# A decoder layer on one core: the first expert's rows, the last batch's norm, the experts' roots and the last gathers moved or rewritten

## The chip, the core and the metric

The kernel runs on one core of one Trainium2 chip. The metric is the time of one execution on the device in microseconds (us), as the median of a few runs. The engines are named as in the profile: PE is TensorE (PEld its weight loads), DVE is VectorE, ACT is ScalarE, POOL is GpSimd, and SP is the sync engine, whose queue issues most of the plain transfers. Every engine takes its own instructions in the order in which they stand in its queue. Durations below come from one profiled execution.

## The reference

The layer has 16 batches of 256 tokens of width 256, all in float32. It has three parts, each followed by a residual sum and a layer norm. The part that the change touches is the third, and the end of the second:

```
# 2: cross attention of the tokens (after norm 1) to 77 context rows and to themselves, 8 heads of 128
sim = q @ k.T ; attn = softmax(sim) ; out = (attn @ v) @ Wo + bo
x = layernorm(x + out)
# 3: experts: each token picks its 2 best of 8 experts; an expert takes its first 512 tokens
dot = x @ embeddings.T ; weights = softmax over the top 2
for each expert e: y = relu(x_e @ first[e].T) @ second[e].T * weight ; final[tokens of e] += y
x = layernorm(x + final)
```

The first part is a recurrence over the sequence with a short convolution ahead of it. It is not touched.

## The kernel before, in words

**Attention.** A loop runs over 128 pairs of batch and head, `(b, h)`, as a software pipeline (L875 to L891). In step i it makes keys and queries of head i (`head_kq`, matmuls `pk`, `pq`), runs the small jobs that a table `steps` has put at that head, multiplies probabilities and values of head i-2 (`head_out`, `po`, L484), makes scores and softmax of head i (`head_softmax`, `s`, L448: a maximum on DVE, two exponentials on ACT, a reciprocal L456 and two scalings L459 on DVE), and transposes the probabilities of head i-1 (`head_turn`, `pa` and `pb`, L471, copied to SBUF by DVE at L473 and by ACT at L474).

**What the table puts where.** At the heads of batch b, the table places the end of batch b-1: the two projections (`project`, `pw`, L502, one per 128 tokens, eight matmuls each), with bias, residual and norm behind the second one (L511 to L516), the transposes of its tokens (`turn_tokens`, `px`), the expert scores (`score_experts`, `pl`, L544), the choice of two experts (`choose`), and `dispatch`. The last counts the tokens per expert with two small matmuls (L611, L612), computes row numbers on DVE (L613 to L646) and scatters every token's row to one table `xg` in DRAM with four indirect transfers on POOL (L649). `settle` scales the tokens again and stores them. Batch 15 has no next batch, so its end runs behind the loop (L892 to L898).

**Experts.** The rows of an expert are a slot. There are nine slots: slot 0 holds the rows of expert 0 out of batches 0 to 14, slot 1 its rows of batch 15 (256 rows at most), slots 2 to 8 the experts 1 to 7. `Rows` loads the rows of a slot from `xg` on SP (L743) and derives on DVE, with 13 small operations (L748 to L775), the weights, the row to add, and the target row. `turn_rows` transposes them (`pe`, L783, copied at L785 by DVE and L787 by ACT), `first_product` multiplies with the first weights (`pi`, L798, relu on ACT at L805), `second_product` with the second (`pf`, L814, scaled on ACT at L821 and stored to a second table, L824). A token's second expert adds the first one's result: `gather` fetches it with up to four indirect transfers on POOL (L834). `finish` sums on DVE (L850, L852), takes mean and variance (L855, L856, L859), raises the variance to the power of -0.5 on POOL (`rsqrt`, L132), normalizes (L863), and scatters the rows to the output on POOL (L864).

**What sets the order.** A scheduler orders each engine's queue from the program order and data dependences when the kernel is built. It moves instructions of independent work past each other, so the order in a queue is not the order of the lines. Around the end of attention, the code creates slot 0's `Rows` in the last loop step that has keys (L880), its `turn_rows` behind `settle` (L900). POOL holds the gathers and scatters in one queue; in slots 2 to 7 it is four gathers, then the slot's four scatters with the pows between them.

Of the kernel before, what the change touches and what calls it, by code (L numbers as in the profile page):

```python
# [10 lines left out]
F32 = mybir.dt.float32  # L11
I32 = mybir.dt.int32
AF = mybir.ActivationFunctionType
ALU = mybir.AluOpType
# [4 lines left out]
P = 128  # L19
B, S, D = 16, 256, 256  # L20
# [10 lines left out]
DC = D // P  # L31
EPS = 1e-5
GT = S // P
OOB = 8192
DX = D + 6
# [3 lines left out]
def decoder_layer(  # L39
# [28 lines left out]
    nc = tc.nc  # L68
    V, A, G, T = nc.vector, nc.scalar, nc.gpsimd, nc.tensor
# [5 lines left out]
    NS = CAP // P  # L75
# [8 lines left out]
    def bank(name, tag="mm", bufs=2):  # L84
        return ps.tile([P, 512], F32, tag=tag, bufs=bufs, name=name)
# [376 lines left out]
    def head_turn(b, h):  # L462

        pn = pns.pop((b, h))
        pt01 = bank(f"pa{b}_{h}", "pa", 1)
        pt2 = bank(f"pb{b}_{h}", "po", 1)
        for jc, (j0, jn) in enumerate(JCS):
            for ic in range(2):
                c0 = (jc % 2) * S + ic * P
                dst = pt01 if jc < 2 else pt2  # L470
                T.transpose(dst[0:jn, c0 : c0 + P], pn[:, ic, j0 : j0 + jn], ident)  # L471
        ptt = b2.tile([P, 3, S], F32, tag="ptt", name=f"ptt{b}_{h}")
        V.tensor_copy(ptt[:, 0:2, :], pt01.rearrange("p (j i) -> p j i", j=2))  # L473
        A.copy(ptt[0:M, 2, :], pt2[0:M, 0:S])  # L474
        ptts[b, h] = ptt

    def head_out(b, h):

# [12 lines left out]

        A.activation(outs_t[b][:, h, :], po[:, 0:S], AF.Identity, bias=bkv_s[:, H + h : H + h + 1])  # L492

    pws, norms = {}, {}

    def project(b, i):

        ot = outs_t[b]
        if i == 0:
            pws[b] = bank(f"pw{b}")  # L500
        for h in range(H):
            T.matmul(  # L502
                pws[b][:, i * D : (i + 1) * D],
                lhsT=ot[:, h, i * P : (i + 1) * P],
                rhs=wo_s[:, h, :],
                start=(h == 0),
                stop=(h == H - 1),
            )
        if i == 0:
            return  # L510
        xb = b1.tile([P, 2, D], F32, tag="xb", name=f"xb{b}")  # L511
        for j in range(2):
            G.tensor_tensor(xb[:, j, :], xs[b][:, j, 0:D], bo_s, ALU.add)  # L513
        y = b2.tile([P, 2, D], F32, tag="yb", name=f"yb{b}")
        V.tensor_tensor(y.rearrange("p i d -> p (i d)"), pws.pop(b), xb.rearrange("p i d -> p (i d)"), ALU.add)  # L515
        norms[b] = layernorm(xs[b], y, 2, P, f"b{b}")  # L516

    def settle(b):

# [8 lines left out]

    def turn_tokens(b):
        x2s[b] = b1.tile([P, DC, S], F32, tag="x2", name=f"x2{b}")  # L530
        pt = bank(f"px2{b}")
        for k in range(DC):
            for i in range(2):
                c0 = k * S + i * P
                T.transpose(pt[:, c0 : c0 + P], xs[b][:, i, k * P : (k + 1) * P], ident)
        V.tensor_copy(x2s[b].rearrange("p k t -> p (k t)"), pt)
# [125 lines left out]
    def at(b, h, f, *args):  # L662
        if 0 <= b < B:
            steps[b, h].append((f, args))
# [4 lines left out]
    for b in range(B):  # L669
        nb = b + 1  # L670
        new_pair = nb % PB == 0 and nb < B
        if b > 0:
            early = int(b == B - 1)
            at(b, 2, project, b - 1, 0)
            at(b, 3, project, b - 1, 1)
            at(b, 5 - early, turn_tokens, b - 1)
            at(b, 6 - early, score_experts, b - 1)
            at(b, 6 - early, choose, b - 1)
            at(b, 7 - early, dispatch, b - 1)
            at(b, 7, settle, b - 1)  # L680
# [42 lines left out]
    LAST = E  # L723
# [11 lines left out]
    class Rows:  # L735


        def __init__(self, e):
            expert, r0, self.n = SLOTS[e]
            code = float(E - expert)  # L740
            self.x = x = e0.tile([P, NS, DX], F32, tag="xe", bufs=3, name=f"xe{e}")
            x = x[:, 0 : self.n, :]
            nc.sync.dma_start(x, xg[r0 : r0 + self.n * P, :].rearrange("(s p) d -> p s d", p=P))  # L743
            narrow = lambda tag, e, dtype=F32: es.tile([P, NS], dtype, tag=tag, name=f"{tag}{e}")[:, 0 : self.n]
            first, token = x[:, :, D + 3], x[:, :, D + 2]

# [79 lines left out]

    gs = {}

    def gather(e):

        R = rows[e]
        gs[e] = e2.tile([P, NS, D], F32, tag="ge", name=f"ge{e}")
        for s in range(R.n):
            G.indirect_dma_start(  # L834
                out=gs[e][:, s, :],
                out_offset=None,
                in_=oe_d[0 : SLOTS[e][1], :],
                in_offset=bass.IndirectOffsetOnAxis(ap=R.at[:, s : s + 1], axis=0),
            )

    def finish(e, y):
        R, g = rows.pop(e), gs.pop(e, None)
# [3 lines left out]
        for a, z in [(0, 2), (2, 3), (3, 4)] if e == LAST else [(a, a + 2) for a in range(0, R.n, 2)]:  # L846
# [10 lines left out]
            n = z - a  # L857
            v = small.tile([P, n], F32, tag="v", name=f"ve{e}_{a}")
            V.tensor_scalar(v, mv[:, a:z, 1], EPS, None, ALU.add)  # L859
            r = rsqrt(v, n, P, f"e{e}_{a}")  # L860
            for s in range(a, z):
                i = slice(s - a, s - a + 1)
                V.tensor_scalar(o[:, s, :], us[s], mv[:, s, 0:1], r[:, i], ALU.subtract, ALU.mult)  # L863
# [12 lines left out]
    for i in range(len(heads) + 2):  # L876
        if i == len(heads) - 2 * H:
            rec.close()
            open_early()
        if i == len(heads) - 1:  # L880
            rows[0] = Rows(0)
        if i < len(heads):
            head_kq(*heads[i])
            for f, args in steps[heads[i]]:
                f(*args)
        if i >= 2:
            head_out(*heads[i - 2])
        if i < len(heads):
            head_softmax(*heads[i])
        if 1 <= i <= len(heads):  # L890
            head_turn(*heads[i - 1])  # L891
    project(B - 1, 0)  # L892
    project(B - 1, 1)
    turn_tokens(B - 1)
# [2 lines left out]
    dispatch(B - 1)  # L897
    settle(B - 1)  # L898

    turn_rows(0)  # L900
    work.close()
    e2 = ctx.enter_context(tc.tile_pool(name="e2", bufs=2))
    load_expert(1, e2)
# [1 line left out]
    for e in range(LAST + 1):  # L905
        it = first_product(e)
        if e < LAST:
            rows[e + 1] = Rows(e + 1)
            turn_rows(e + 1)
        y = second_product(e, it)  # L910
        if e < LAST:
            gather(e + 1)
        finish(e, y)
        if 2 <= e < E - 1:
            load_expert(e + 1, e2)

# [49 lines left out]
```

## Time and profile before

| | |
|---|---|
| median of 3 runs | 1229.26 us (1229.24 to 1230.31) |
| the profiled execution | 1232.08 us, of it the span of the trace 1230.4 us |
| PE, DVE, ACT, POOL busy | 96%, 59%, 40%, 22% of the span |
| mean granted PE clock | 0.988 |
| last attention matmul (`po`) ends, last projection ends | 1075.97, 1080.69 us |
| slot 1's first transpose, last `pf` block begins | 1102.31, 1209.36 us |
| last scatter begins, trace ends | 1226.17, 1230.4 us |

The span runs from the first to the last instruction that the profiler saw; the profiled execution's own time is 1.7 us longer than its span. Busy means that an instruction of the engine was running, not that it ran at its peak. In a line of an engine's timeline stand the start in us, the duration in us, the engine, the line of the kernel, the operation, what it writes and reads, how many instructions were merged, and in brackets the idle time before it and what ended it. A line of windows has the stretch, its length, the busy time and count of PE, PEld, DVE, ACT and POOL, the granted PE clock, the DMA engines' busy share and GB/s. In the chain of waits stand start, length and what ran.

### The profile page before, as it was taken

How to read it: one execution, taken by the hardware profiler on the slowest of the kernel's cores; microseconds unless marked ns; L12 is line 12 of the kernel's file. 1: busy time of each engine (PE TensorE's matmuls, PEld its weight loads, DVE VectorE, ACT ScalarE, POOL GpSimd, SP SyncE). 2: the span in 40 equal slices, each digit the busy share in tenths (PEclk: the TensorE clock that was granted, in tenths of full speed). 3: DMA queues.
4: the chain of work that ended last, by engine and by line, in shares of the span. 5: the costliest groups of instructions: out<-in, count | busy, mean ns of one | idle time of the engine just before them, and what ended most of it. 6: DMA issues, size and time to landing. Idle time of an engine off the chain costs nothing.

```text
span 1230.4 us, 15284 instructions
## 1 busy us (share of the span) xinstructions
PE 1187.3 (96%) x5000; PEld 842.3 (68%) x5000; DVE 725.9 (59%) x2122; ACT 489.4 (40%) x1270; POOL 274.5 (22%) x500
## 2 busy tenths in 40 slices
PE   7799999999999999999999999999999999889995
PEld 3356777767776777677767776777677778756663
DVE  6535755684558555756486548564766464555654
ACT  3135434443435344534353434443543344313331
POOL 3200021122111311131111210221021112135566
PEclk9899999999999999999999999999999999999998
DMA  8730100010001100010000000000001000146762
GB/s 262 245 107 1 37 18 29 9 54 18 29 9 32 37 11 20 26 37 5 19 21 28 12 19 19 22 9 14 9 13 43 13 9 3 29 146 147 177 158 82
DMA packets 43617, 60.80 MB, mean 49 GB/s; under 512 B 7945, under 2 KB 31414, under 8 KB 43538
## 3 DMA queue, kind: packets, MB, share of 16 engines
q1 hardware_dynamic: 36674, 50.34, 12.8%
q0 software_dynamic: 6144, 9.48, 3.3%
q8 instruction: 39, 0.64, 0.2%
q14 instruction: 40, 0.33, 0.1%
q10 hardware_dynamic: 720, 0.01, 0.0%
HBM read 36.55 MB, written 30.78 MB: 55 GB/s over the span
## 4 chain that ended last, share of the span: by engine, by line
PE 82%; DVE 7%; POOL 3%; issue 3%; DMA 3%; ACT 1%; POOLq 0%; SPq 0%; DVEq 0%
PE po L484 12%; PE pk L433 10%; PE s L448 10%; PE pw L502 9%; PE pq L438 8%; PE pv L413 8%; PE ph L281 5%; PE pa L471 4%; PE pi L798 3%; PE pvc L365 3%; PE px L301 2%; PE pf L814 2%; PE pb L471 2%; PE pl L544 1%; DMA xe<-xg 1%
## 5 line engine op out<-in xcount | busy, mean ns | idle before, releaser
L450 DVE TENSOR_REDUCE nm<-s 128x2 f32<-128x666 f32 x128 | 108.4, 847 | 144.7 <-PE s L448 144.4
L484 PE MATMUL po<-ptt,v 128*128 128x256 f32 (+1 forms) x768 | 190.2, 382 | 2.2 <-DVE ptt L473 2.2
L484 PEld LDWEIGHTS po<-ptt,v 128*128 128x128 f32 (+1 forms) x768 | 144.2, 191 | 57.1 <-issue 32.7
L433 PE MATMUL pk<-kvt,wkv_s 128*128 128x333 f32 x512 | 165.1, 444 | 0.0
L448 PE MATMUL s<-kt,qt 128*128 128x333 f32 x512 | 164.4, 442 | 0.0
L492 ACT ACTIVATE ot<-po,bkv_s 128x256 f32<-128x256 f32 x128 | 60.6, 474 | 235.4 <-PE po L484 235.3
L454 ACT ACTIVATE p<-s,nm 128x333 f32<-128x333 f32 x256 | 135.1, 534 | 37.9 <-DVE nm L450 28.6
L438 PE MATMUL pq<-kvt,wq_s 128*128 128x256 f32 x512 | 131.2, 379 | 0.0
L413 PE MATMUL pv<-wkv_s,kvt 128*128 128x512 f32 x256 | 121.6, 599 | 0.0
L448 PEld LDWEIGHTS s<-kt,qt 128*128 128x128 f32 x512 | 96.5, 189 | 31.2 <-ACT qt L440 0.5
L438 PEld LDWEIGHTS pq<-kvt,wq_s 128*128 128x128 f32 x512 | 96.7, 189 | 30.5 <-issue 0.5
L474 ACT COPY ptt<-pb 77x256 f32<-77x256 f32 x128 | 47.1, 368 | 177.3 <-PE pb L471 175.9
L502 PE MATMUL pw<-wo_s,ot 128*128 128x256 f32 x512 | 117.2, 381 | 0.0
L502 PEld LDWEIGHTS pw<-wo_s,ot 128*128 128x128 f32 x512 | 97.4, 191 | 13.4 <-ACT ot L492 0.2
L433 PEld LDWEIGHTS pk<-kvt,wkv_s 128*128 128x128 f32 x512 | 87.6, 191 | 23.0
L459 DVE TENSOR_SCALAR pn<-p,rs 128x333 f32<-128x333 f32 x256 | 93.1, 397 | 4.2
L471 PEld LDWEIGHTS pa<-ident,pn 128*128 128x128 f32 x512 | 63.5, 141 | 38.7 <-DVE pn L459 11.1
L649 POOL DMA_INDIRECT xg<-xs,sidx x64 | 67.3, 1052 | 93.1 <-DVE sidx L646 78.4
L473 DVE COPY ptt<-pa 128x512 f32<-128x512 f32 x128 | 87.3, 682 | 0.9 <-PE pa L471 0.6
L513 POOL TENSOR_TENSOR xb<-xs,bo_s 128x256 f32<-128x256 f32 x32 | 21.2, 684 | 283.4 <-DVE yb L515 283.4
L471 PE MATMUL pa<-ident,pn 128*128 128x128 f32 x512 | 78.8, 274 | 5.9 <-DVE pn L459 5.9
L290 DVE SCALAR_TENSOR_TENSOR cv<-hp,cw,cv 128x512 f32<-128x512 f32 x96 | 71.4, 749 | 2.0
(167 smaller groups left out, 1596.4 us busy)
## 6 DMA issues: line engine op xcount, KB each, us to landing
v<-vc SPq DMA_DIRECT2D x16, 308.0 KB
vc<-vc SPq DMA_DIRECT2D x9, 512.0 KB
xg<-zero SPq DMA_DIRECT2D x17, 262.0 KB
xe<-xg SPq DMA_DIRECT2D x8, 524.0 KB
xT<-in_xT SPq DMA_DIRECT2D x8, 512.0 KB
xt<-in_x_in SPq DMA_DIRECT2D x16, 256.0 KB
out<-o SPq DMA_DIRECT2D x16, 256.0 KB
w<-in_w1T SPq DMA_DIRECT2D x8, 512.0 KB
```

The source lines that it names most:

```text
L290: V.scalar_tensor_tensor(cv, hp[:, :, k : k + S], cw[:, c, k : k + 1], cv, ALU.mult, ALU.add)
L413: T.matmul(pv, lhsT=kvts[b][:, k, jc * P : (jc + 1) * P], rhs=wkv_s[:, k, INNER + f0 : INNER + f0 + 512], start=(k == 0), stop=(k == DC - 1),)
L433: T.matmul(pk[:, 0:J], lhsT=wkv_s[:, k, f], rhs=kvt[:, k, :], start=(k == 0), stop=(k == DC - 1))
L438: T.matmul(pq[:, 0:S], lhsT=wq_s[:, k, f], rhs=kvt[:, k, 0:S], start=(k == 0), stop=(k == DC - 1))
L448: T.matmul(s[:, ic, 0:J], lhsT=qt[:, ic * P : (ic + 1) * P], rhs=kt, start=True, stop=True)
L450: V.tensor_reduce(nm, s[:, :, 0:J], AX.X, ALU.max, negate=True)
L454: A.activation(p[:, ic, :], s[:, ic, 0:J], AF.Exp, bias=nm[:, ic : ic + 1], accum_out=sm[:, ic : ic + 1])
L459: V.tensor_scalar(pn[:, ic, :], p[:, ic, :], rs[:, ic : ic + 1], None, ALU.mult)
L471: T.transpose(dst[0:jn, c0 : c0 + P], pn[:, ic, j0 : j0 + jn], ident)
L473: V.tensor_copy(ptt[:, 0:2, :], pt01.rearrange("p (j i) -> p j i", j=2))
L484: T.matmul(po[:, 0:S], lhsT=vs[b][0:jn, jc, h * DH : (h + 1) * DH], rhs=ptt[0:jn, jc, :], start=(jc == 0), stop=(jc == 2),)
L502: T.matmul(pws[b][:, i * D : (i + 1) * D], lhsT=ot[:, h, i * P : (i + 1) * P], rhs=wo_s[:, h, :], start=(h == 0), stop=(h == H - 1),)
```

## The change

It has four parts.

1. **The first expert's rows.** `Rows` is split: making one only issues the load, the new method `read` holds the 13 DVE operations. Slot 0's load is created one loop step earlier, its transposes in the last step with keys, and its `read` one step later, with an edge that puts it behind the DVE copy of the last head (L473). At the heads of batch 15 the work of batch 14 moves up: both projections at head 2, transposes at head 3, scores and choice at head 4, dispatch at head 5.
2. **The last batch by halves.** For batch 15, each half of 128 tokens has its own PSUM bank and its own norm behind its projection (`norm_half`); the transposes of a half go to a bank of their own and are copied apart.
3. **The experts' norms.** In all slots but slot 0 the power of -0.5 on POOL is replaced by a square root on ACT, a reciprocal on DVE and one Newton step of three operations on DVE (`root`).
4. **The last gathers.** In slot 7 an edge puts the POOL instructions of `finish`, its scatters, behind the gathers of slot 8.

```diff
-        V.tensor_copy(ptt[:, 0:2, :], pt01.rearrange("p (j i) -> p j i", j=2))
+        turned = V.tensor_copy(ptt[:, 0:2, :], pt01.rearrange("p (j i) -> p j i", j=2))
...
+        return turned
...
-        if i == 0:
-            pws[b] = bank(f"pw{b}")
+        if i == 0 or b == B - 1:
+            pws[b] = bank(f"pw{b}_{i}")
...
+        if b == B - 1:
+            norm_half(b, i)
+            return
...
+    def norm_half(b, i):
+
+        if i == 0:
+            xbs[b] = b1.tile([P, 2, D], F32, tag="xb", name=f"xb{b}")
+            for j in range(2):
+                G.tensor_tensor(xbs[b][:, j, :], xs[b][:, j, 0:D], bo_s, ALU.add)
+            norms[b] = [small.tile([P, 2] + k, F32, tag=t, name=f"{t}l{b}") for t, k in (("mvl", [2]), ("rl", []))]
+        mv, r = norms[b]
+        y = b2.tile([P, D], F32, tag="yl", name=f"yl{b}_{i}")
+        V.tensor_tensor(y, pws[b][:, i * D : (i + 1) * D], xbs[b][:, i, :], ALU.add)
+        st = small.tile([P, 6], F32, tag="st", name=f"stl{b}_{i}")
+        V.bn_stats(st, y)
+        V.bn_aggr(mv[:, i, :], st)
+        v = small.tile([P, 1], F32, tag="vl", name=f"vl{b}_{i}")
+        V.tensor_scalar(v, mv[:, i, 1:2], EPS, None, ALU.add)
+        G.tensor_tensor(r[:, i : i + 1], v, nhalf[:, 0:1], ALU.pow)
+        V.tensor_scalar(xs[b][:, i, 0:D], y, mv[:, i, 0:1], r[:, i : i + 1], ALU.subtract, ALU.mult)
...
+        if b == B - 1:
+
+            for i in range(2):
+                pt = bank(f"px2{b}_{i}", "pk" if i == 0 else "pq", 1)
+                for k in range(DC):
+                    T.transpose(pt[:, k * P : (k + 1) * P], xs[b][:, i, k * P : (k + 1) * P], ident)
+                V.tensor_copy(x2s[b][:, :, i * P : (i + 1) * P], pt[:, 0:D].rearrange("p (k t) -> p k t", k=DC))
+            return
...
-            early = int(b == B - 1)
+            early = 2 * int(b == B - 1)
             at(b, 2, project, b - 1, 0)
-            at(b, 3, project, b - 1, 1)
+            at(b, 3 - early // 2, project, b - 1, 1)
...
+        def read(self, e):
...
+    def root(v, n, name):
+
+        q = es.tile([P, n], F32, tag="qe", name=f"qe{name}")
+        A.activation(q, v, AF.Sqrt)
+        i0 = es.tile([P, n], F32, tag="ie", name=f"ie{name}")
+        V.reciprocal(i0, q)
+        i2 = es.tile([P, n], F32, tag="i2", name=f"i2{name}")
+        V.tensor_tensor(i2, i0, i0, ALU.mult)
+        t = es.tile([P, n], F32, tag="te", name=f"te{name}")
+        V.scalar_tensor_tensor(t, i2, -0.5, v, ALU.mult, ALU.mult)
+        r = es.tile([P, n], F32, tag="re", name=f"re{name}")
+        V.scalar_tensor_tensor(r, t, 1.5, i0, ALU.add, ALU.mult)
+        return r
...
-            r = rsqrt(v, n, P, f"e{e}_{a}")
+            r = rsqrt(v, n, P, f"e{e}_{a}") if e == 0 else root(v, n, f"{e}_{a}")
...
-        if i == len(heads) - 1:
+        if i == len(heads) - 2:
             rows[0] = Rows(0)
...
-            head_turn(*heads[i - 1])
+            turned = head_turn(*heads[i - 1])
+        if i == len(heads) - 1:
+            turn_rows(0)
+        if i == len(heads):
+            with tc.issue_after(turned.ins):
+                rows[0].read(0)
...
-    turn_rows(0)
...
             rows[e + 1] = Rows(e + 1)
+            rows[e + 1].read(e + 1)
             turn_rows(e + 1)
         y = second_product(e, it)
-        if e < LAST:
-            gather(e + 1)
-        finish(e, y)
+        gathered = gather(e + 1) if e < LAST else None
+        if e == LAST - 1:
+
+            with tc.issue_after(gathered.ins):
+                finish(e, y)
+        else:
+            finish(e, y)
```

More of the change, by code (lines that the diff above doesn't have):

```diff
@@ L492, in head_out @@
         A.activation(outs_t[b][:, h, :], po[:, 0:S], AF.Identity, bias=bkv_s[:, H + h : H + h + 1])
-    pws, norms = {}, {}
+    pws, norms, xbs = {}, {}, {}
     def project(b, i):
         ot = outs_t[b]
-        if i == 0:
-            pws[b] = bank(f"pw{b}")
+        if i == 0 or b == B - 1:
+            pws[b] = bank(f"pw{b}_{i}")
         for h in range(H):
@@ L738, in __init__ @@
         def __init__(self, e):
-            expert, r0, self.n = SLOTS[e]
+            _, r0, self.n = SLOTS[e]
+            self.x = e0.tile([P, NS, DX], F32, tag="xe", bufs=3, name=f"xe{e}")
+            nc.sync.dma_start(
+                self.x[:, 0 : self.n, :], xg[r0 : r0 + self.n * P, :].rearrange("(s p) d -> p s d", p=P)
+            )
+        def read(self, e):
+            expert, r0, _ = SLOTS[e]
             code = float(E - expert)
-            self.x = x = e0.tile([P, NS, DX], F32, tag="xe", bufs=3, name=f"xe{e}")
-            x = x[:, 0 : self.n, :]
-            nc.sync.dma_start(x, xg[r0 : r0 + self.n * P, :].rearrange("(s p) d -> p s d", p=P))
+            x = self.x[:, 0 : self.n, :]
             narrow = lambda tag, e, dtype=F32: es.tile([P, NS], dtype, tag=tag, name=f"{tag}{e}")[:, 0 : self.n]
@@ L833, in gather @@
         for s in range(R.n):
-            G.indirect_dma_start(
+            last = G.indirect_dma_start(
                 out=gs[e][:, s, :],
@@ L839, in gather @@
             )
+        return last
     def finish(e, y):
```

## Prediction

> **What bounds the kernel now.** I read the page's 40 slices (30.8 us each) first:
>
> ```profile
> PE   7799999999999999999999999999999999889995
> ```
>
> TensorE (PE) is 90% busy or more in all but the first two, slices 35 and 36 (1046 to 1107 us) and the last. Elsewhere a lighter VectorE or GpSimd pays nothing. Then I read the chain of waits from 1040 us on, and there each engine's timeline. Three stretches are not PE work, and the change goes to each.
>
> First, the end of the last attention head. The chain says what starts it, VectorE (DVE) and PE what it costs:
>
> ```profile
> 1062.45 2.17 DMA xg<-xs,sidx
> 1064.63 4.32 DMA xe<-xg
> ```
>
> ```profile
> 1069.04 0.17 DVE L748 TENSOR_TENSOR dw<-xe 128x4 f32<-128x4 f32 x1 [3.76 <-DMA xe<-xg]
> ...
> 1069.91 0.16 DVE L456 RECIPROCAL rs<-sm 128x2 f32<-128x2 f32 x1
> ...
> 1080.73 0.69 DVE L515 TENSOR_TENSOR yb<-pw,xb 128x512 f32<-128x512 f32 x1 [8.52 <-PE pw L502]
> ...
> 1087.16 0.17 DVE L552 COPY lg<-pl 128x16 f32<-128x16 f32 x1 [1.15 <-PE pl L544]
> ```
>
> ```profile
> 1070.63 0.84 PE L471 MATMUL pa<-ident,pn 128*128 128x128 f32 x4 [3.59 <-DVE pn L459]
> ...
> 1102.31 1.03 PE L783 MATMUL pe<-ident,xe 128*128 128x128 f32 x4 [3.18 <-DMA xe<-xg]
> ...
> 1209.36 7.07 PE L814 MATMUL pf<-w,it 128*128 128x256 f32 x32
> ```
>
> DVE takes its queue in order. L748 (expert rows, not needed for 30 us) waits for the load; the last softmax's reciprocal stands behind it, though its exps were done at 1065.95. PE loses 3.59 us, then runs slow:
>
> ```profile
> 1070.00:1072.00 2.00, 1.37 (x8) 1.11 (x9) 1.36 (x8) 0.00 (x0) 0.00 (x0) 0.93 0.00 0
> 1072.00:1074.00 2.00, 2.00 (x7) 1.64 (x7) 0.20 (x1) 0.37 (x1) 0.00 (x0) 0.50 0.00 0
> 1074.00:1076.00 2.00, 2.00 (x8) 1.66 (x7) 0.00 (x0) 0.00 (x0) 0.00 (x0) 0.72 0.00 0
> ```
>
> The column before the last two is the granted clock. Second, the path from the last projection (1080.69) through norm, routing, scatter and load of slot 1's rows to 1102.31; PE has filler, but 3.18 us too little. Third, behind PE's last block (from 1209.36) GpSimd's (POOL's) queue ends last:
>
> ```profile
> 1167.35 0.99 POOL L834 DMA_INDIRECT ge<-oe,at  x1 [0.30 <-issue]
> ...
> 1183.52 0.99 POOL L834 DMA_INDIRECT ge<-oe,at  x1 [0.30 <-issue]
> ...
> 1212.23 0.99 POOL L834 DMA_INDIRECT ge<-oe,at  x1 [0.30 <-issue]
> ...
> 1226.17 1.02 POOL L864 DMA_INDIRECT out<-oe,to  x1 [0.74 <-DVE oe L863]
> ```
>
> Gathers and scatters take turns on it, about 1.28 us each with the pause. The first two lines are the first gathers of slots 5 and 6, the third those of slot 8, behind three scatters of slot 7; the last is the kernel's last scatter, and the span ends 4.2 us behind its start.
>
> **Part 1, rows behind the head, batch 14 one head earlier.** Moved: both projections of batch 14 into head 2, its turn, scores and dispatch one head up, with their four scatters; the load of slot 0's rows follows them. On POOL they go into 13.58 us of idle before the first scatter; on SP (the sync queue) the load keeps its place between two output stores. Head 5's projections then end near 1050.5 (head 2's at 1027.16, plus 6.88 of projection, 0.44 turn, 0.79 scores and three heads' other work, about 5.1 each). The counts (L611, L612) end at 1050.85 for 1056.06 before, 5.2 earlier; the load lands near 1063.8 for 1069.0. In the changed build's PE list slot 0's eight transposes stand right behind pb of head 6, which ends at 1064.28: 0.5 us of slack. The wait is new, on PE, with everything behind it; its cost lies between 0 and, if routing is a microsecond later than shifted, 1 us. I take 0, as the shift uses measured rows.
>
> Then PE has no hole: 1064.28 + 0.87 (8 transposes of 0.109) + 6.88 (16 projection matmuls of 0.43) + 2.6 (two po) + 0.66 (pa, pb) = 1075.3 for 1080.69. Of the 5.4 us, 3.59 is the hole, the rest slow clock and a wait for pn. The 13 row instructions (1.1 us of DVE) go behind L473 of the last head, where DVE idled 8.52.
>
> **Part 2, last batch by halves.** Half 0 is normed under half 1's projection (3.44 us of PE; its chain of add 0.42, statistics 0.61, 0.15, pow 0.58 and scale 0.42 with hops takes 2.5), so it costs nothing. From the end of half 1: add 0.42, half 0's copy 0.42, statistics 0.61, eps 0.15, pow 0.58, scale 0.42 and hops end at 2.9. PE meanwhile has px 0.22, a pi 0.87, pl 0.4, two pi 1.75 = 3.24, then the second px 0.22, pi 0.87, pl 0.4: logits at 4.85, for 6.47 before. Gain 1.6; the same pi matmuls stand in front as cover, and without it the gain would be up to 2.5. Behind the logits all lengths stay (15.1 us to 1102.3), as the weight loads, whose wait ends with the last pl, move along. So slot 1 starts 5.4 + 1.6 = 7.0 us earlier, at 1095.3. PE's filler ends at 1091.2, a hole of 4.1 us for 3.18.
>
> [...] The trace decides: after 3.18 us the next 4 us were granted 0.61 and 0.54. The price is paid already, so I add nothing[...].
>
> **Part 3, root and Newton step.** Sixteen pows (0.71 each) leave POOL; sixteen square roots (0.20, by the row of the equally small exp) go to ScalarE (ACT), 64 small operations (0.17) to DVE. From variance to scale it was 0.94 (1174.96 to 1175.90 in slot 5); now 0.28 to ACT and back (as df to den in the routing) and four dependent steps of 0.2, 1.1. In the changed build's DVE list work on the next u stands between them, so the first scale comes some 1.2 us later, the second pair 0.4. Slots 2 to 7 are PE's: 7.02 + 0.87 + 6.91 = 14.8 us each, and DVE is 56% busy, so this is hidden as long as no queue holds PE.
>
> ACT's queue could: each root waits for a variance, hence for gathers, and behind the second root of a slot stand three relus PE needs. With a slot's pf start as zero, PE waits if that variance (L859) starts later than about 13.8: the next pf starts at 14.8 and uses the last relu 1.3 later, after three matmuls of 0.43; root and three relus of 0.6 take 2.05, and 0.25 goes to the variance and a hop. Before, it stood at 13.3, 13.8 and 13.7 in slots 5 to 7 (1179.13 - 1165.82, 1194.42 - 1180.62, 1209.09 - 1195.43), because POOL's loop (1167.35 to 1183.52, mean 15.7) is longer than PE's. In the changed list the fourth scatter of each slot stands behind the next gathers: 15.7 + 0.4 - 1.3 = 14.8, so no drift. Slot 3's gathers, at -0.3 before, then stand at -1.2, and the variance follows gathers by 11.1 (mean of slots 4 to 7): near 10 to 11. I take 0; bounds 0 and 3 us (0.9 a slot from slot 5).
>
> [...] But the changed list has one new load, ahead of slot 1's root and behind the last exp; the trace's only load takes 1.28, and ACT idles 2.07 at that place between two relus. By row 0[...]; I take 0.
>
> **Part 4, last gathers first.** Slot 8's gathers wait only for slot 7's last store: its last ye ends 7.6 us into that slot's pf, and with about 2.2 to land (as xg above) that is near 4 us before the last pf block. Slot 7's four scatters queue behind the four gathers, to about 6.3 us into that block (8 of 1.28). Nothing reads what they write. With the block's start as zero, slot 8's scatters are then bound by DVE: the first variance at 6.0 (as in slot 2, which waits for matmul results, not gathers), re 7.75, oe to 8.7, the last add 8.8, its statistics to 10.5, variance 10.95, root and three steps to 12.07, oe 0.4, hop 0.33: last scatter at 12.8, for 16.8 before (1226.17 - 1209.36). Gain 4.0. Next late is this DVE chain; were POOL bound again, 1.3 a place in the queue.
>
> **Sum.** 7.0 + 4.0 = 11.0. Profiled execution: span 1230.4 to 1219.4, its own 1232.08 to 1221.1. That lies 2.8 above the median of 1229.26, from which I subtract: 1218.3, taken as 1218.5 with the first wait's small risk.
>
> **Rivals.** (a) ACT's roots hold PE: the loop stays at 15.7 to 16, variance passes 13.8 from slot 5, 2 to 3.5 us come back: 1220.5 to 1222. For it: 13.8 was reached before. Against: the scatter out of the loop. (b) The rows land after 1064.3, or the pi cover takes the half gain: 1 to 2.5 back, about 1220. For: 0.5 us of slack. Against: both shifts are of measured rows. (c) The tail gains 2.5 only, as root steps stretch on DVE: 1220. (d) Slower: the mechanism of (a) in every slot. It decides once the loop exceeds 16.6 (six slots of 1.8 eat 11); at 17.1, three more, about 1232. For it: the loops of slots 2 and 3 were 16.9 and 16.8 (in slot 3 PE itself waited 0.76 for ACT's ye). Against: they held one scatter more. (e) The moves cancel and the time stays within 0.2%, about 1228: the moves would have to miss the engines' queues, and the changed build's lists show them there.
>
> **Chances.** Main 0.62; (a) 0.14; (b) 0.10; (c) 0.07; (d) 0.03; (e) 0.04. Range 1215.5 (slot 3's hold of 0.9 gone and slack used) to 1223.5. Faster by over 0.2% (what this measurement can tell, 2.5 us) 0.93, same 0.04, slower 0.03.
>
> **What would show it.** Right: no idle before pa of the last head and clock 1.0 there; logits near 1080; slot 1's transposes near 1095; blocks of 14.8 us; last scatter 12.8 behind the last block's start. Wrong: a wait of PE for xe near 1064, relus waiting behind roots with PE idle before pf, more than one new table load, POOL busy without pause to the end.

## The result, and the profile after

The changed kernel takes 1219.81 us (median of 4 runs, 1219.65 to 1220.79) for 1229.78 (4 runs, 1229.24 to 1230.93): 10.0 us less, a ratio of 0.9919 with an interval from 0.9903 to 0.9934. The prediction was 1218.5. The profiled execution took 1219.74 us, its span 1218.0, which is 12.4 below the span of the profiled execution before; why that is more than 10.0 is part of what follows.

First the slices again, PE's row of the page of the kernel after:

```profile
PE   7799999999999999999999999999999999989996
```

Slice 35, an 8 before, is full now; slice 36 is left, with the hole ahead of slot 1. Now the end of attention, in PE's timeline and then DVE's:

```profile
1063.19 0.38 PE L471 MATMUL pb<-ident,pn 128*77 128x128 f32 x2
1063.41 1.04 PE L819 MATMUL pe<-ident,xe 128*128 128x128 f32 x8
...
1066.01 0.60 PE L471 MATMUL pa<-ident,pn 128*128 128x128 f32 x4
...
1069.27 5.34 PE L503 MATMUL pw<-wo_s,ot 128*128 128x256 f32 x24
```

```profile
1065.11 0.17 DVE L456 RECIPROCAL rs<-sm 128x2 f32<-128x2 f32 x1
...
1067.26 0.16 DVE L784 TENSOR_TENSOR dw<-xe 128x4 f32<-128x4 f32 x1
...
1079.35 0.17 DVE L582 COPY lg<-pl 128x16 f32<-128x16 f32 x1 [0.78 <-PE pl L574]
```

No bracket stands before slot 0's transposes (`pe`) or before `pa` of the last head: the hole of 3.59 us is gone. The reciprocal runs ahead of the row operations (`dw`), which come without a wait. The projections end at 1074.61 (69.27 + 5.34), the logits start 4.74 us later. Then slot 1, and the clock behind its hole in windows of 2 us (the granted clock stands before the last two columns):

```profile
1094.70 1.11 PE L819 MATMUL pe<-ident,xe 128*128 128x128 f32 x4 [4.31 <-DMA xe<-xg]
```

```profile
1072.00:1074.00 2.00, 2.00 (x11) 1.76 (x10) 0.83 (x4) 0.00 (x0) 0.58 (x1) 1.00 0.00 0
1094.00:1096.00 2.00, 1.21 (x5) 0.81 (x5) 1.24 (x13) 0.15 (x1) 0.94 (x1) 0.50 0.95 258
1096.00:1098.00 2.00, 2.00 (x5) 1.64 (x6) 1.16 (x9) 0.22 (x1) 0.84 (x2) 0.50 1.08 376
1098.00:1100.00 2.00, 2.00 (x6) 1.55 (x6) 1.08 (x12) 0.67 (x2) 1.70 (x2) 0.50 0.34 117
1100.00:1102.00 2.00, 2.00 (x13) 1.77 (x12) 1.20 (x13) 0.83 (x3) 1.39 (x3) 1.00 0.42 49
```

The clock is whole at 1072, where it was 0.50 before, and half from 1094 to 1100, the first 5.3 us behind the hole. Last, POOL behind the last `pf` block, which begins at 1201.58:

```profile
1198.12 0.97 POOL L884 DMA_INDIRECT ge<-oe,at  x1 [4.95 <-DMA oe<-ye]
...
1203.15 1.01 POOL L915 DMA_INDIRECT out<-oe,to  x1 [0.30 <-issue]
...
1209.96 0.97 POOL L915 DMA_INDIRECT out<-oe,to  x1 [1.94 <-DVE oe L914]
...
1213.89 0.97 POOL L915 DMA_INDIRECT out<-oe,to  x1 [0.39 <-DVE oe L914]
```

The last scatter stands 12.31 us behind the block's start, for 16.81.

**All kernels by stage.** The table is worked out from the starts and ends in the timelines of the profiled executions, those of the experiments below among them (three kernels, which are told at their place, are left out). The first column starts at the end of `pb` of head 6; up to there these kernels do nearly the same work. "Slots" runs from slot 1's `pf` to slot 8's; seven slots without a wait of PE make 99.25.

| kernel | pb to last projection | to logits | to slot 1's pe | pe to pf of slot 1 | slots | last pf to last scatter |
|---|---|---|---|---|---|---|
| before | 16.25 | 6.47 | 15.15 | 6.78 | 100.27 | 16.81 |
| before, again | 15.79 | 6.47 | 15.32 | 7.99 | 99.25 | 15.85 |
| part 1 alone | 11.04 | 6.65 | 15.31 | 7.46 | 99.51 | 18.56 |
| without halves | 11.04 | 6.65 | 15.29 | 7.44 | 101.04 | 14.88 |
| without roots | 11.04 | 4.74 | 15.30 | 6.70 | 100.13 | 15.78 |
| without the last order | 11.04 | 4.74 | 15.16 | 6.70 | 102.86 | 12.86 |
| after | 11.04 | 4.74 | 15.35 | 7.63 | 99.25 | 12.31 |
| after, again | 11.04 | 4.74 | 15.33 | 6.62 | 102.30 | 13.97 |
| after, third | 11.04 | 4.74 | 15.22 | 6.70 | 99.25 | 12.29 |
| after, idle products and ACT copies | 11.04 | 4.73 | 15.20 | 5.33 | 99.25 | 12.30 |
| the same without roots | 11.04 | 4.74 | 15.20 | 5.33 | 99.26 | 15.79 |

The last three columns jump by about 1 us and more between executions of one kernel too. "Before" against "after" differs by 5.21 + 1.73 - 0.20 - 0.85 + 1.02 + 4.50 = 11.4, and 0.87 that after's execution was ahead of before's when head 6 ended; "before, again" against "after, third" by 4.75 + 1.73 + 0.10 + 1.29 + 0 + 3.56 = 11.4 and 0.22. So 10.0 to 11.4 of the change are in parts 1 and 2 and in the tail; the clock and the slots add or take up to 1.3 us each by chance.

**Where the clock falls.** The clock's share of that chance can be read in the traces. Eleven of them have a hole of 3 to 4.3 us ahead of slot 1, and the half clock behind it lasts one stretch of 3.41 us or two. With one stretch, the clock fell at the hole's end, from 0.2 us ahead of slot 1's first transpose to 0.4 behind it; with two, it fell 0.8 to 1.9 us ahead, while PE was still idle. A window of 1 us in the hole of the kernel after (two stretches), then the same of its third run below (one):

```profile
1093.00:1094.00 1.00, 0.00 (x0) 0.00 (x0) 0.79 (x3) 0.00 (x0) 0.70 (x2) 0.58 0.88 249
```

```profile
1093.00:1094.00 1.00, 0.00 (x0) 0.00 (x0) 0.93 (x4) 0.00 (x0) 0.86 (x1) 1.00 0.85 227
```

### The profile page after: what moved, and what is told of

Its sections match the earlier page's. It is cut to its first block, busy times and chain, and to the rows that moved or that the text cites. A ratio compares the mean times of both kernels' runs of the same rounds, so it can differ in the third digit from the quotient of the medians.

```text
span 1218.0 us, 15325 instructions
## 1 busy us (share of the span) xinstructions
PE 1183.9 (97%) x5000; PEld 841.5 (69%) x5000; DVE 735.0 (60%) x2189; ACT 494.7 (41%) x1287; POOL 263.2 (22%) x485
## 3 DMA queue, kind: packets, MB, share of 16 engines
q1 hardware_dynamic: 36674, 50.34, 12.8%
## 5 line engine op out<-in xcount | busy, mean ns | idle before, releaser
L503 PE MATMUL pw<-wo_s,ot 128*128 128x256 f32 x512 | 115.9, 379 | 0.0
L473 DVE COPY ptt<-pa 128x512 f32<-128x512 f32 x128 | 87.4, 683 | 0.9 <-PE pa L471 0.6
```

Source lines behind the costliest of these rows:

```text
L473: turned = V.tensor_copy(ptt[:, 0:2, :], pt01.rearrange("p (j i) -> p j i", j=2))
L503: T.matmul(pws[b][:, i * D : (i + 1) * D], lhsT=ot[:, h, i * P : (i + 1) * P], rhs=wo_s[:, h, :], start=(h == 0), stop=(h == H - 1),)
```

## The experiments

They ran in three sessions of four, each on another chip, and are compared with the kernel before of their session: 1232.48, 1231.15 and 1230.34 us. The kernel after was run again in the second and third, since the first showed that a comparison across chips misleads here.

My theory going in was that of the prediction, with one addition: the longer hole ahead of slot 1 costs about 1 us of clock. The rivals were that the roots cost something, that the roots and not the last order shorten the tail, and that the missing microsecond goes elsewhere.

**Part 1 alone** (halves, roots and last order taken back):

```diff
-        if i == 0 or b == B - 1:
+        if i == 0:
...
-            r = rsqrt(v, n, P, f"e{e}_{a}") if e == 0 else root(v, n, f"{e}_{a}")
+            r = rsqrt(v, n, P, f"e{e}_{a}")
...
-        if e == LAST - 1:
-
-            with tc.issue_after(gathered.ins):
-                finish(e, y)
-        else:
-            finish(e, y)
+        finish(e, y)
```

> The kernel before with the first part alone (slot 0's rows read behind the last head, batch 14 one head earlier). My theory: the projections end 5.4 us sooner as in the kernel after, but the hole before slot 1 grows with it (its own work on TensorE, the first and second product of slot 0, is shorter now than the way from the projections to slot 1's rows), the clock starts slot 1 at 0.5 for some 6 us instead of 0.6 for 4, and that takes back about 1 us: 1225.4 (1224.5 to 1226.0). Rival, that the 5.4 us come through whole: 1224.4 or less. Rival, that most of the gain is the tail's and the first part gives under 3 us: 1227 or more.

1228.98 us (1226.58 to 1229.88), 0.997 of before (0.9959 to 0.9982): 3.5 us less, under the 4.4 expected. The table says where the rest is: the projections do end 4.75 to 5.2 us sooner and slot 1 starts 4.6 to 4.9 sooner, but the tail takes 18.56 for 15.85 to 16.81. With the powers on POOL its loop over the slots is longer than PE's 14.8 a slot, and POOL carries the end. That loop does start earlier with PE: slot 2's first gather is at 1113.63, 4.3 to 4.8 us sooner than in the two profiles of before. It then runs longer, 15.9 us a slot for 15.7 and 15.4, and slot 8's first gather, at 1209.09, is only 1.9 to 3.1 sooner. Of what is lost, 1.2 us lies at slot 2 (18.13 us to the next slot's first gather, for 16.91 in both profiles of before), where one of ACT's copies came 1.2 us late; such late copies are told below. The kernel before has no profile on this chip, so whether the change or the chip made the rest of the loop longer stays open.

**Without halves.** The same first hunk as above, and `norm_half` and the split transposes not used.

> The kernel after with batch 15 normed and turned whole, as before. My theory: the logits come 1.6 us later and slot 1 starts 1.6 us later, with the hole before it at 5.9 us for 4.31; the clock is already down after 4.31 us, so nothing more is lost to it: 1221.4. Rival, that a longer hole costs more clock: 1222.0 or more. Rival, that the halves gave nothing because the hole's clock took it back: 1219.8 to 1220.3.

1227.66 us (1225.7 to 1228.87), 0.9964 (0.9951 to 0.9977). The logits come 6.65 behind the projections for 4.74, so the halves are worth 1.9 us there, and the hole is 4.18 us, not 5.9: slot 0's own products wait with the path. The hole's clock took two stretches (7.44). The rest of the distance to the kernel after is in the slots (101.04) and the tail, where this run has the late copies told below, so the total decides nothing.

**Without roots** (the second hunk above alone).

> The kernel after with the powers back on GpSimd in every slot. My theory: no instruction of the roots lies on the path of the blocks, which are 14.8 us either way, so the same within 0.7 us, 1219.3 to 1220.5, with the last scatter 12 to 13.5 us behind the last block's start. Rival, that the roots hold TensorE or ScalarE somewhere: 1218 or less. Rival, that the tail's gain needs the roots (the powers stand behind scatters in GpSimd's queue): 1221.5 or more, with the whole loss behind the start of the last block.

1224.62 us (1224.16 to 1225.6), 0.994 (0.9927 to 0.9952). PE's slots lose 0.9 us here, with six late copies in them, and nothing in the repeat below, but the last scatter is 15.78 behind the last block's start. The third case holds, and with it the prediction's division of the gain falls.

**Without the last order** (the third hunk alone).

> The kernel after without the order of the last gathers ahead of the scatters. My theory: the gathers of slot 8 fall behind two of slot 7's four scatters, the last scatter comes at about 16 us behind the start of the last block for 12.3, so 3 to 4.5 us more: 1223 to 1224.3. Rival, that the roots alone bring the tail forward (no powers in GpSimd's queue): within 1 us of the kernel after, 1219.5 to 1220.8.

1224.37 us (1221.63 to 1226.33), 0.9937 (0.9925 to 0.9949). The number is the one that my theory named, and for another reason: its tail is 12.86, only 0.57 over the kernel after. POOL's timeline, with the last block starting at 1204.47:

```profile
1201.66 0.98 POOL L884 DMA_INDIRECT ge<-oe,at  x1 [0.30 <-issue]
...
1208.03 1.00 POOL L915 DMA_INDIRECT out<-oe,to  x1 [0.30 <-DVE ue L903]
1213.41 0.97 POOL L915 DMA_INDIRECT out<-oe,to  x1 [4.39 <-DVE oe L914]
...
1217.33 0.97 POOL L915 DMA_INDIRECT out<-oe,to  x1 [0.39 <-DVE oe L914]
```

Slot 8's gathers do stand behind two of slot 7's scatters, as expected, but POOL then waits 4.39 us for DVE: two places in a queue with that much slack cost nearly nothing. Against slots without a wait 3.6 us were lost, and they were lost in the slots. That was new.

**The kernel after again**, to see whether the slots' loss belongs to the variants.

> The kernel after itself, beside its variants on one chip. The first four variants ran 3.5 to 8.1 us below the kernel before of their chip where 4.4 to 10 were expected, and in two of them TensorE stood 0.3 to 1.5 us before the last second product of most slots, waiting for ScalarE's copy of the second. Theory A, that this hold comes with the variants (their later start moves gathers and scatters against the products): the kernel after stays about 10 us below the kernel before, 0.991 to 0.993, with slots of 14.8 us. Theory B, that it comes and goes with the execution or the chip and the roots only let it last: 0.993 to 0.995, with holds of 0.3 us or more in its slots.

1224.53 us (1223.39 to 1226.34), 0.9952 (0.994 to 0.9965): theory B. The unchanged kernel after gains only 6.6 us on this chip, and PE waits in four of its slots. ACT, POOL and PE in slot 4 of this run, then ACT and PE at the same place of the third:

```profile
1144.53 5.35 PE L850 MATMUL pf<-w,it 128*128 128x256 f32 x24
...
1146.46 0.48 ACT L857 ACTIVATE ye<-pf,we 128x256 f32<-128x256 f32 x1 [1.14 <-PE pf L850]
1147.55 0.95 POOL L884 DMA_INDIRECT ge<-oe,at  x1 [0.30 <-issue]
...
1149.57 0.47 ACT L857 ACTIVATE ye<-pf,we 128x256 f32<-128x256 f32 x1 [2.64 <-PE pf L850]
1150.10 1.99 PE L850 MATMUL pf<-w,it 128*128 128x256 f32 x8 [0.22 <-ACT ye L857]
1151.05 0.48 ACT L857 ACTIVATE ye<-pf,we 128x256 f32<-128x256 f32 x1 [1.01 <-PE pf L850]
```

```profile
1142.34 7.07 PE L850 MATMUL pf<-w,it 128*128 128x256 f32 x32
...
1144.27 0.47 ACT L857 ACTIVATE ye<-pf,we 128x256 f32<-128x256 f32 x1 [1.14 <-PE pf L850]
...
1146.00 0.47 ACT L857 ACTIVATE ye<-pf,we 128x256 f32<-128x256 f32 x1 [1.25 <-PE pf L850]
...
1147.72 0.47 ACT L857 ACTIVATE ye<-pf,we 128x256 f32<-128x256 f32 x1 [1.25 <-PE pf L850]
```

On time, the copies (`ye`) follow each other by 1.73 us. Here the second comes 3.11 behind the first, though PE runs through its 24 matmuls without a break and ACT is idle. By its bracket ACT waits for PE's semaphore, which then came 1.4 us late; that something else, which the trace does not show, held ACT is not ruled out. The fourth `pf` needs the second copy's bank, so PE stands for it, 0.22 by the bracket and some 0.5 in start to start (slots of 15.3). I call these late copies. ACT's queue has no root between these two copies. The first profile of before has one as well, in slot 3, with no root in the kernel:

```profile
1140.76 0.84 ACT L821 ACTIVATE ye<-pf,we 128x256 f32<-128x256 f32 x2 [3.09 <-PE pf L814]
```

It is 1.95 us behind the modelled end of its matmuls, and the wait of PE there, 0.76, is the one that the prediction's rival (d) mentions.

**Idle products in the hole.** To test the clock term, nine matmuls that nobody reads were put into the hole (`last_pf` is the last matmul of slot 0's second product; slot 1's rows are turned behind them):

```diff
-            turn_rows(e + 1)
+            if e > 0:
+                turn_rows(e + 1)
...
+        if e == 0:
+            pd = bank("pd", "pa", 1)
+            with tc.issue_after(last_pf[0].ins):
+                for k in range(9):
+                    dummy = T.matmul(pd[:, 0:256], lhsT=ident, rhs=w1_s[0][:, 0, 0:256], start=True, stop=True)
+            with tc.issue_after(dummy.ins):
+                turn_rows(1)
```

> The kernel after with nine matrix products of 256 columns that nobody reads, put on TensorE between slot 0's second product and slot 1's rows: 4.0 us of work in the hole of 4.3. My theory: the half clock after the hole comes from TensorE's idleness, so the granted clock stays 1.0, slot 1's first product takes 3.6 to 4.0 us for 5.7, and the second product of slot 1 starts 1.7 to 2.7 us sooner: 1.5 to 2.7 us below the kernel after on the same chip. Rival, that the clock drops for another cause or the filling delays slot 1's rows: within 0.5 us of the kernel after, or slower.

1229.09 us (1226.09 to 1231.86, 17 runs), 0.9984 (0.9976 to 0.9991): 4.6 slower than the kernel after beside it. The hole is filled and `pe` takes 0.66 us for 1.11, at full clock. But the later place of `turn_rows` in the program put its DVE copy behind slot 0's last norm and the reading of the next rows in DVE's queue:

```profile
1090.86 4.05 PE L974 MATMUL pd<-w,ident 128*128 128x256 f32 x18
1095.05 0.66 PE L819 MATMUL pe<-ident,xe 128*128 128x128 f32 x4
1099.44 6.07 PE L834 MATMUL pi<-xet,w 128*128 128x256 f32 x16 [3.74 <-DVE xet L821]
```

A new hole of 3.74 us, and 6.07 for the product at half clock behind it: the rival that the filling delays slot 1's rows held. This says nothing against the clock term; it is the old head-of-line wait of slot 0 made again by hand.

**Gathers behind scatters.** In slots 0 to 6 the next slot's gathers go behind all four scatters:

```diff
+        if e < LAST - 1:
+            last_out = finish(e, y)
+            with tc.issue_after(last_out.ins):
+                gather(e + 1)
...
+            continue
```

> The kernel after with the gathers of slot e+1 behind all four scatters of slot e in GpSimd's queue, for every slot but the last pair: the round of gathers, sums, root and scatters becomes longer than the 14.8 us of a slot. My theory (the point from which the slower rival decides): the variance of the second pair drifts from 10 us behind the start of the second product to more than 13.8, and from then on ScalarE, whose root stands ahead of the next copy, holds TensorE: slots of 16 to 17 us, the whole 3 to 10 us above the kernel after. Rival, that the loop still fits: slots of 14.8 and within 1 us of the kernel after.

1227.82 us (1226.48 to 1228.98), 3.3 above the kernel after beside it, and 103.19 us for the seven slots. The 3.3 is not the price of the hold, though it lies in the theory's 3 to 10: the kernel after lost 3.05 us in its slots here to late copies, and this kernel has none of them before slot 8, so the slots differ by only 0.9; 2.6 stand in the tail (16.57 for 13.97), where slot 8's last copy came 5 us late. The price is what the slots lose against 99.25, 3.9 us. Gathers start 16.6, 16.4, 15.9, 14.9 and 15.9 us apart. The hold is there, but only one slot reaches the 16 to 17 us expected (slot 4, 17.2), and it is at the first pair's root, not the second's. ACT and PE in slot 4, whose `pf` began at 1143.82:

```profile
1154.66 0.20 ACT L868 ACTIVATE qe<-ve 128x2 f32<-128x2 f32 x1 [4.98 <-DVE ve L910]
1154.77 0.46 ACT L857 ACTIVATE ye<-pf,we 128x256 f32<-128x256 f32 x1
1155.12 0.59 ACT L841 ACTIVATE it<-pi 128x512 f32<-128x512 f32 x1
```

```profile
1155.76 1.55 PE L834 MATMUL pi<-xet,w 128*128 128x512 f32 x3 [2.30 <-ACT it L841]
```

The root waits 4.98 us; the last copy and the first relu stand behind it, and PE waits for the relu's bank. The first variance stood 8.6, 10.6, 8.9 and 8.7 us behind `pf` in slots 3, 4, 6 and 7, and PE's waits were 0.25, 2.30, 0.60 and 0.35: each is that distance less 8.3. In slot 5 it stood at 8.2 and PE did not wait. So 8.3 is the point for the first pair. In the kernel after (third run) it stood at 5.8 to 7.1.

**Reading not held back.** Slot 0's load still comes a head earlier, but its row operations may stand anywhere in DVE's queue:

```diff
-            with tc.issue_after(turned.ins):
-                rows[0].read(0)
+            rows[0].read(0)
```

> The kernel after without the order that holds the reading of slot 0's rows behind the last head's turn: its small operations stand on VectorE's queue ahead of head 6's normalising again, as in the kernel before, but their rows are now loaded a head earlier. My theory: VectorE waits for nothing long, the 13 small operations of 0.07 us cost about 1 us ahead of the last heads' softmax, TensorE has a hole of 0.5 to 1.5 us before head 6's turn: 0.5 to 1.5 us above the kernel after. Rival, that the place in the queue and not the earlier load cures the hole: 3 us or more above the kernel after, with a hole of 3 us and the clock at a half behind it.

1226.92 us (1224.67 to 1227.94), 2.4 above the kernel after beside it. Nine of the row operations stand ahead of a reciprocal again, now head 6's, and the first of them waits for the load:

```profile
1063.84 0.17 DVE L784 TENSOR_TENSOR dw<-xe 128x4 f32<-128x4 f32 x1 [3.38 <-DMA xe<-xg]
...
1064.64 0.16 DVE L456 RECIPROCAL rs<-sm 128x2 f32<-128x2 f32 x1
```

PE's timeline shows

```profile
1065.29 0.84 PE L471 MATMUL pa<-ident,pn 128*128 128x128 f32 x4 [1.25 <-DVE pn L459]
```

where the kernel after has no wait. The hole is in my range and the clock stays whole, but the cause is not the one I named: DVE does wait for the load. From the end of head 5's `pa` to that of head 6's `pb` it takes 6.9 us for 5.3. The rest of the 2.4 is not the place's: the clock took two stretches behind slot 0's hole for one (7.62 us from `pe` to `pf` for 6.62). So of part 1's 4.75 to 5.2 us the place behind the head brings 1.6 where the load is early, and the earlier load the rest; the place without the earlier load was not run.

**The third session** had no late copy in any of its four profiles.

> The kernel before, for one profiled look on the chip of these runs. In the kernel after and its variants ScalarE's copy of a slot's second product was released 1.0 to 2.0 us behind the end of that product's last matrix product as TensorE's rows show it, about 2.1 us behind the start of the last of a run of gathers or scatters on GpSimd, and TensorE stood 0.2 to 1.5 us for it. Theory, that this is of the execution and the roots only decide which slots it strikes: the kernel before shows such late copies here too, but a hold of TensorE in fewer slots, so that its eight later slots are within 1.5 us of 14.8 each. Rival, that it comes with the roots: no late copy here.

1230.54 us (one run). No late copies with or without roots, so this run couldn't tell the two apart: the theory's first half, that they would show on this chip, was wrong.

> The kernel after once more, as the ground of the next two on one chip. Two sessions gave 0.9919 and 0.9952 of the kernel before. Theory (late copies differ from session to session): again between 0.991 and 0.996. No rival.

1219.6 us (1218.82 to 1220.57), 0.9916 (0.9902 to 0.9929): 10.7 less than before, as in the first comparison.

The idle products once more, with both copies of slot 1's turned rows on ACT:

```diff
-            if k == 0:
+            if k == 0 and e != 1:
                 V.tensor_copy(xet[:, k, 0 : n * P], pt[:, 0 : n * P])
```

> The nine idle matrix products in the hole before slot 1 again, with both turned halves of slot 1's rows copied by ScalarE, so that the copy no longer stands behind slot 0's sums on VectorE, which cost the first trial a hole of 3.7 us. My theory: the clock stays at 1.0 over slot 1, its first product takes 3.6 to 4.2 us, and slot 1's second product starts 1.7 to 2.7 us sooner than in the kernel after: the whole 1.0 to 2.7 us below the kernel after on the same chip. Rival, that the clock falls all the same or another wait takes the place: within 0.7 us or slower.

1217.75 us (1217.1 to 1218.33), 0.9896 (0.988 to 0.9911): 1.85 below the kernel after beside it, and the fastest kernel of the study. PE, then two windows of the clock:

```profile
1091.29 4.05 PE L974 MATMUL pd<-w,ident 128*128 128x256 f32 x18
1095.61 0.66 PE L819 MATMUL pe<-ident,xe 128*128 128x128 f32 x4 [0.27 <-DMA xe<-xg]
1096.51 3.72 PE L834 MATMUL pi<-xet,w 128*128 128x256 f32 x16 [0.24 <-ACT xet L823]
```

```profile
1094.00:1096.00 2.00, 1.73 (x11) 1.23 (x9) 1.27 (x8) 0.00 (x0) 1.70 (x2) 1.00 0.88 226
1096.00:1098.00 2.00, 1.76 (x10) 1.36 (x9) 1.34 (x15) 0.97 (x3) 0.74 (x2) 1.00 1.03 330
```

The kernel after beside it, with one stretch of half clock, has

```profile
1094.74 1.12 PE L819 MATMUL pe<-ident,xe 128*128 128x128 f32 x4 [4.17 <-DMA xe<-xg]
1095.94 4.78 PE L834 MATMUL pi<-xet,w 128*128 128x256 f32 x16
```

The clock stays whole with the idle products, and slot 1's rows to its `pf` take 5.33 for 6.70, 1.4 less. The ACT copies bring none of it: PE waits 0.24 us for them, and the kernel after waits for no copy there. The 1.4 is under the 1.7 to 2.7 that I expected of this stage.

> The same with the powers back on GpSimd in place of the roots. Theory A, that the roots cost nothing and bring nothing: within 0.8 us of the run with roots. Theory B, that the roots, by the place in which they put gathers and scatters beside the second products, let late copies hold TensorE 0.5 us in each slot from the third on: 1 to 3 us below the run with roots, with slots of 14.8 to 15.0. Theory C, that the powers cost the tail: 1 us or more above, all of it behind the start of the last second product.

1221.6 us (1220.27 to 1223.41), 0.9929 (0.9915 to 0.9943): 3.85 above the same with roots, theory C. Slots of 99.26 either way; the tail is 15.79 for 12.30, 3.5 of the 3.85. POOL's queue to the end:

```profile
1208.18 0.74 POOL L132 TENSOR_TENSOR re<-ve,nhalf 128x2 f32<-128x2 f32 x1
1209.66 1.04 POOL L917 DMA_INDIRECT out<-oe,to  x1 [0.74 <-DVE oe L916]
...
1214.38 0.58 POOL L132 TENSOR_TENSOR re<-ve,nhalf 128x1 f32<-128x1 f32 x1
1215.70 1.04 POOL L917 DMA_INDIRECT out<-oe,to  x1 [0.74 <-DVE oe L916]
```

Each power takes its own 0.58 to 0.74 us on the queue of the scatters, and then the queue stands 0.74 for the scaling that needs the power. It also has to wait for its turn behind the scatters of slot 7. With roots, slot 8's four scatters start 1.28 to 1.36 us apart, and the first of them 1.4 us sooner behind the block's start.

## Why the prediction was right, point by point

The time was right within 1.3 us, inside the range. Of the steps behind it one was wrong in what it credited, and two chances were left out.

- **Part 1, 5.4 us.** 5.2 in the first pair of profiles, 4.75 in the second. The slack of 0.5 us for the load held: no kernel shows a wait there. Reading the queue order out of DVE's timeline was enough; the run without the held reading, where DVE's wait for the load comes back ahead of a reciprocal, confirms it from the other side. (`pb` of head 6 ends at 1064.45 before, not at 1064.28; the sum from there to the last projection, 11.0, was right: 11.04.)
- **Part 2, logits at 4.85, gain 1.6.** 4.74, gain 1.73; the terms that the prediction lists make 4.73. The hole ahead of slot 1 was to be 4.1 us and was 4.31 and 4.17.
- **The clock behind the hole, "the price is paid already, so I add nothing".** The trace of before had one stretch of half clock there. In truth there are one or two, each 3.41 us long, and the length of the hole did not say which: holes of 3.18, 4.10, 4.12, 4.17, 4.25 and 4.29 us had one, of 3.36, 4.18, 4.20 (twice) and 4.31 had two. From `pe` to `pf` of slot 1 it takes 6.6 to 6.9 with one, 7.4 to 8.0 with two, and 5.33 with none. What did say it, in all eleven traces, is where in the hole the clock fell. So nothing is to be added for a longer hole, but a comparison of two executions carries about 1 us of chance from it; against the single profile of before it came out 0.85 worse, in the next pair 1.29 better. In the profile of before the falls behind the two holes are 30.72 us apart, nine stretches of 3.413; what sets the place of a fall was not shown. The shortest holes, of 3.18 and 3.21 us, were followed by a stretch too.
- **Part 3, cost 0.** Right where PE is concerned, in the one session without late copies that has both: 99.25 us with roots, 99.26 without. Between slots 3 and 7 the loop came out at 14.5 to 15.3 for the 14.8 predicted. The one new table load took 1.28 us (at 1108.32), as in the trace's row; the relu ahead of it ends at 1108.30 and the root starts at 1109.61, so ACT stands neither ahead of it nor behind it. The limit for ACT's hold was placed at the wrong root: the first pair decides, at 8.3 us behind `pf`, which rival (d) should have named.
- **Part 4, "last scatter at 12.8, for 16.8 before. Gain 4.0".** Measured 12.3, and 3.5 to 4.5. The size and the next-late work (DVE's chain of the last rows) were right. The step that failed is the credit: the sum of 12.8 was made with the roots in place, and the prediction put all of it down to the order of the gathers. With the roots and without the order the tail is 12.86; with the order and without the roots 15.79. So with the order in place 3.5 us come from the roots, and with the roots in place 0.6 or less from the order. Without the roots the order brings 0.06 to 1.0 against the two profiles of before, and 2.8 against part 1 alone on the same chip, a comparison that late copies cloud. What was overlooked is that a power on POOL cost the queue twice, its own time (0.58 to 0.74 us) and the wait for the scaling behind it (0.74). Part 3 was called hidden because no row of PE changed; that it shortens the queue that sets the end was in the same profile (the 0.71 and the bracket of 0.74 before each scatter), and was not read.
- **Where 11.0 became 10.0.** The parts add up to 5.2 + 1.7 + 4.5 = 11.4 by the first profiles and 10.0 by the second (4.75, 1.73, 3.56); the medians say 10.0 and 10.7. Before's profiled execution was 2.8 us above its median, with slots 1.0 longer (0.76 of it the wait in slot 3) and a tail 1.0 longer than in its next profile; the slower clock of that next profile takes 1.2 back.
- **Not foreseen: late copies.** They came in every profile of two of the four sessions, and in the first profile of before; in the one of these sessions where the kernel after ran, it took 1224.53 us for 1219.8. Rival (a), that PE is held at ACT, thus came true there, but by a late release, not by a root ahead of the copy. They struck kernels with and without roots (four times in part 1 alone, which has powers), so the roots are not what makes them. Whether roots let them weigh more, by the place in which they put the gathers, isn't settled: in those two sessions PE waited 0.2 us in the kernel without roots and 0 in part 1 alone, for 1.2 to 2.7 in those with roots, but no two kernels that differ in the roots alone ran on one chip with late copies. There the gain in the tail may be gone: from slot 1's `pf` to the last scatter it took 115.9 us without roots, 115.7 without the order, 115.9 without halves and 116.3 in the kernel after, for 111.6 in the kernel after without late copies. The 3.5 us of the roots are measured only where no copy is late.

## What to carry to other kernels

An operation on the queue that also issues the last transfers was paid twice here, in its own time (0.58 to 0.74 us) and in the wait of the queue for the operation's consumer on another engine (0.74); look there before you call a change hidden. Credit a gain to a part only after a sum, or a run, that leaves the part out: here one variant hit its number for a wrong reason, and only its timeline told. Where PE had to wait 4.2 us anyway, idle matmuls that kept its clock were worth 1.4 to 1.9 us, provided that moving code for them didn't reorder another engine's queue (where it did, the kernel was 4.6 us slower than the kernel after).

## What the runs showed of the hardware

- The half clock came in stretches of 3.41 us, one or two behind a wait of PE of 3.2 to 4.3 us: one where the clock fell at the end of the wait (0.2 us ahead to 0.4 behind, and 1.1 behind at the head of before), two where it fell 0.8 to 2.0 us ahead of it. Waits of 1.25 us (head 6) to 2.30 us (slot 4 of the kernel with late gathers) left the clock whole.
- Late copies: ACT's copy started 0.4 to 2.7 us behind the modelled end of the matmuls that it waits for (once 5 us), in 59 of 67 cases 2.0 to 2.6 us behind the start of one of POOL's indirect transfers (1149.57 for the gather at 1147.55). They came in every kernel of two sessions (with the late gathers only in slot 8), four times in the first profile of before, and in none of the other five profiles, whose POOL issues the same transfers. In those stretches the trace names some releasers no more ("issue" stands where the third run's brackets name PE). What delays the copy was not found, and whether it is of the chip or of the session wasn't tried.
